# A mixture-of-experts kernel: three partial sums instead of four, base rows and fc2 fetched among the expert slots, each row turned ahead of the prior row's products

## The chip, the core and the metric

The kernel runs on one core of one Trainium2 chip. A core has five engines that run side by side, each with its own instruction queue: TensorE (PE, matrix products; its weight loads appear as PEld), VectorE (DVE), ScalarE (ACT), GpSimd (POOL) and SyncE (SP), which here only issues transfers. Sixteen DMA engines move data between the DRAM and the on-chip memory (128 partitions). The metric is the device time of one execution in microseconds (us); the median of three runs is given.

## What is computed

A sequence model layer on x of 4 rows of 512 tokens with 512 channels: a bidirectional decay scan (WKV), an attention-like time mix and channel mix, a second scan, and then a feed-forward part with 32 experts, of which each token uses 8. The change touches only how the experts' results are summed and added in. In the reference:

```python
# x: tokens x 512; topi, wsel: the 8 experts of each token and their weights
cw = zeros((T, E)).at[arange(T)[:, None], topi].add(wsel)
x_lat = x @ fc1_w.T                                  # 256 wide
h = relu2(einsum('tl,eil->eti', x_lat, w1))
h = h * cw.T[:, :, None]
y_lat = einsum('eti,eli->tl', h, w2)
routed = y_lat @ fc2_w.T                             # 512 wide
shared = relu2(x @ shared_up_w.T) @ shared_down_w.T
return shared + routed
```

The layer's output is x plus this. The kernel holds everything that is added to `routed` (x, the mixes and `shared`) in DRAM as `base_dram`, four rows of 512 tokens, transposed: channels on the partitions.

## The kernel before

**Order of the work.** From 0 to about 757 us the scans, the mixes, the routing and the shared expert run; their instruction orders are written out by hand. The routing scatters each token's latent row once per chosen expert into `x_dram`, grouped by expert (line 672), with the token's number in the last column. Then come the expert slots, then the end. Within the slots only VectorE's order is written by hand; in the end no engine's is. Elsewhere a scheduler places instructions by priority (program order) and readiness, and it may move a transfer far ahead of its place in the program where SP has nothing more urgent.

**The slots** (`pairs`, line 1148). A pair is two tiles of 128 rows. `fetch` (line 1058) loads the rows as `xg` on SP, into a ring of six buffers: the first 16 pairs (`MIXED`) by two loads, later ones by one. `slots` (line 1105) runs a pair through four steps, and three pairs are in work at a time: turn `xg` on TensorE and copy it to `xt`; first product (`h_ps`) and relu; square; second product (`y_ps`), scaled by the routing weight into `yo` (line 1138). GpSimd then adds each of the two tiles of 128 rows of 256 values to a sum in DRAM by an indirect DMA that accumulates (line 1140). There are four sums (`SUMS`), and pair i, tile j goes to sum (2i + j) mod 4. A scatter waits until the one before it on the same sum has landed. Padding rows carry token numbers from `ROWS` on, so they land behind the 2048 real rows. 74 pairs always run (`SURE`); six more lie in a conditional block (line 1166), which these inputs skip. The branch not taken makes up the semaphores that the block would have counted, on GpSimd after all scatters have landed (an instruction that ends at 1065.14 us).

**The end** (line 1171). `fc2` and three base rows are loaded (lines 1172 to 1177; the fourth's buffer holds expert weights until the slots are over). For each of four rows b: four loads of the sums (line 1186, tokens spread so that partition p gets tokens p, 128 + p, 256 + p, 384 + p, hence 1 KB pieces), three additions (line 1192), eight turnings on TensorE (`lt`, line 1196), a copy to `yl` by ScalarE (line 1200), sixteen products with `fc2` (line 99, called from 1205), two additions of the base (line 1207), two stores (line 1208).

**Where the buffers lie.** The pool `ep` of the slots begins where the pools `cpool` and `bp` of the earlier stages lay, and a buffer of it may be written once what was there is no longer used. The offsets in bytes within a partition, as the program of before has them:

| earlier stage | slots and end |
|---|---|
| `z` 153568 to 161760 | `xg`, six buffers, 153568 to 167560 (pair 0: 153568) |
| `lat`, two, 161760 to 171024 | |
| `side` 171040 to 191520 | `xt`, two: 167584 and 169632 to 171680 |
| | `ht` 171680, `hr` 175776 (two each), `yo` 179872 (six) to 192160 |
| `rstd` 191520 to 193568 | `index`, nine, 192160 to 192448 |
| `sh` 193568 to 201760 | `w1`, two: 192448 and 194496; `fc2` 196544 |
| `fg`, small ones, `sw`, `zeros`, tables: 201760 to 228384 | `base0` 200640, `base1` 208832, `base2` 217024 to 225216 |

A tag's buffers stand together, and `w1` is first asked for at pair 16. `side` holds intermediate results of the shared expert for the last rows and is stored by ScalarE's queue at 751.3 and 758.2 us (line 721). The profile leaves out digits at the end of names: `w1` is `w`, `fc2` is `fc`, and `base0` is `base`.

Of the kernel before, what the change touches and what calls it, by code (L numbers as in the profile page):

```python
# [29 lines left out]
F32 = mybir.dt.float32  # L30
AF = mybir.ActivationFunctionType
ALU = mybir.AluOpType
# [3 lines left out]
B = 4  # L36
# [13 lines left out]
SURE = 74  # L50
MIXED = 16
WIDTH = 256 + E + 1
SUMS = 4
EXP30 = math.exp(30.0)
UNIT = NC * T

# [9 lines left out]
def model_kernel(ctx: ExitStack, tc: tile.TileContext, a: dict, out: bass.AP):  # L66
# [200 lines left out]

    x_dram = dram.tile([E * REGION + 3 * P, WIDTH], F32, tag="x_dram", name="x_dram")

    sum_dram = [dram.tile([ROWS + P, 256], F32, tag=f"sum{i}", name=f"sum{i}") for i in range(SUMS)]  # L270


    z_dram = [dram.tile([NC, P, T], F32, tag=f"z{b}", name=f"z{b}") for b in range(B)]
# [482 lines left out]
    def clear_tails():  # L756


        zeros = bp.tile([P, WIDTH], F32, tag="zeros", name="zeros")
        nc.vector.memset(zeros, 0.0)  # L760
        nc.gpsimd.iota(
            zeros[:, 256 + E : 257 + E], [[0, 1]], base=ROWS, channel_multiplier=1,
            allow_small_or_imprecise_dtypes=True,
        )
        for i in range(3):

            if i < 2:
                spare = x_dram[E * REGION : E * REGION + 2 * P, :].rearrange("(p j) n -> j p n", j=2)[i]
            else:
                spare = x_dram[E * REGION + 2 * P :, :]  # L770
            s = nc.gpsimd.dma_start(spare, zeros)
            tc.declare_no_dep(s.ins, group="scatter", reason="no two write one row")
            tc.add_to_no_dep_group("scatter", s.ins)
        yield
        ps = acc_tile()
        nc.tensor.matmul(ps[:1, 0, :E], lhsT=ones[:, 0:1], rhs=seen, start=True, stop=True)
        tail = bp.tile([1, E], F32, tag="tail", name="tail")
        nc.vector.tensor_tensor(tail, ps[:1, 0, :E], region[:1, :], ALU.add)
        ends = bp.tile([1, E], mybir.dt.int32, tag="ends", name="ends")
        nc.vector.tensor_scalar(ends, tail, -1.0, None, ALU.add)  # L780
        yield
        for e in range(E):
            _, (row,) = nc.values_load_multi_w_load_instructions(
                ends[0:1, e : e + 1], engines=[mybir.EngineType.SP], min_val=0, max_val=E * REGION,
                skip_runtime_bounds_check_because="a region has room for every row and a slot's tail",
            )
            s = nc.sync.dma_start(x_dram[bass.ds(row, P), :], zeros)
            tc.declare_no_dep(s.ins, group="scatter", reason="no two write one row but with zeros")
            tc.add_to_no_dep_group("scatter", s.ins)
            if e % 4 == 3:  # L790
                yield
# [112 lines left out]
    def clear_sum(i, j):  # L904

        s = sum_dram[i]
        if j < 2:
            nc.sync.dma_start(s[j * ROWS // 2 : (j + 1) * ROWS // 2, :].rearrange("(p r) n -> p (r n)", p=P), zero)
        else:
            nc.sync.dma_start(s[ROWS:, :], zero[:, :256])  # L910

    sums = iter([(i, j) for j in range(3) for i in range(SUMS)])

# [124 lines left out]
    with (  # L1038
# [19 lines left out]
        def fetch(i):  # L1058
            xg = ep.tile([P, 2, WIDTH], F32, tag="xg", name="xg", bufs=6)
            rows = of_pair(2, i, ET.SP, E * REGION)  # L1060
            if i < MIXED:
                for j, row in enumerate(rows):
                    nc.sync.dma_start(xg[:, j, :], x_dram[bass.ds(row, P), :])
            else:

                nc.sync.dma_start(xg, x_dram[bass.ds(rows[0], 2 * P), :].rearrange("(p j) n -> p j n", j=2))
            return xg
# [37 lines left out]
        def slots(i, xg):  # L1105
            ps = turn(xg, "xt_ps")
            xt = tile4("xt", [2, 2, P])
            if i < MIXED:
                nc.vector.tensor_copy(xt, ps)  # L1109
            else:  # L1110
                nc.scalar.copy(xt, ps)

                w1 = tile4("w1", [2, 256])
                o = of_pair(0, i, ET.Activation, (E - 1) * (UNIT // 2))[0]
                nc.scalar.copy(w1.rearrange("p k n -> p (k n)"), big[:, bass.ds(o, 512)])  # L1115
            yield
            at = of_pair(0, i, ET.PE, (E - 1) * (UNIT // 2))
            h = tile4("ht", [2, 2, P])
            if i < MIXED:
                ps = rows_times(xt, at, 0, "h_ps")  # L1120
                r = tile4("hr", [2, 256])
                nc.scalar.activation(r, ps, AF.Relu)
                yield
                ps = turn(r, "ht_ps")
                nc.scalar.activation(h, ps, AF.Square)
            else:
                ps = inner(xt, w1)
                r = tile4("hr", [2, 256])
                nc.scalar.activation(r, ps.rearrange("p m j r -> p m (j r)"), AF.Relu)  # L1129
                yield  # L1130
                nc.vector.tensor_tensor(h.rearrange("p m j r -> p m (j r)"), r, r, ALU.mult)  # L1131
            yield
            ps = rows_times(h, at, 1, "y_ps")
            y = tile4("yo", [2, 256], bufs=6)
            index = ep.tile([P, 2], mybir.dt.uint32, tag="index", name="index", bufs=9)
            nc.vector.tensor_copy(index, xg[:, :, 256 + E])
            for j, column in enumerate(of_pair(1, i, ET.DVE, 256 + E - 1)):
                nc.vector.tensor_scalar(y[:, j, :], ps[:, j, :], xg[:, j, bass.ds(column, 1)], None, ALU.mult)  # L1138

                nc.gpsimd.indirect_dma_start(  # L1140
                    out=sum_dram[(2 * i + j) % SUMS][:, :],
                    out_offset=bass.IndirectOffsetOnAxis(ap=index[:, j : j + 1], axis=0),
                    in_=y[:, j, :], in_offset=None,
                    bounds_check=ROWS + P - 1, compute_op=ALU.add,
                )
            yield

        def pairs(first, end):

            live = []  # L1150
            with tc.manual_schedule(engines={ET.DVE}):
                for i in range(first, end + 3):
                    if i < end:
                        live.append(slots(i, fetch(i)))
                    for s in live:
                        next(s, None)
                    if len(live) > 3:
                        live.pop(0)
# [9 lines left out]
        slot_psum.close()  # L1168


        fc2 = tile4("fc2", [2, C], bufs=1)
        nc.sync.dma_start(fc2, a["fc2"])
        base = []
        for b in range(B):
            base.append(tile4(f"base{b}", [NC, T], bufs=1) if b + 1 < B else chunked(views(13, UNIT, 1)[0]))
            if b + 1 < B:
                nc.sync.dma_start(base[b], base_dram[b][:, :, :].rearrange("c p t -> p c t"))
        got = Ring([v.rearrange("p (t n) -> p t n", t=NT) for v in views(1, NT * 256, 4 * SUMS)])
        lat_t = Ring([chunked(v, 2) for v in views(10, 2 * T, 2)])
        res_ring = Ring([chunked(v, 2) for v in views(11, 2 * T, 4)])  # L1180
        with tc.tile_pool(name="fpsum", bufs=2, space=bass.MemoryType.PSUM, reuse_waits="tile") as fps:
            for b in range(B):
                parts = []
                for s in sum_dram:
                    g = got()
                    nc.sync.dma_start(g, s[b * T : (b + 1) * T, :].rearrange("(t p) n -> p t n", p=P))
                    parts.append(g)
                if b + 1 == B:
                    nc.sync.dma_start(base[b], base_dram[b][:, :, :].rearrange("c p t -> p c t"))
                while len(parts) > 1:  # L1190
                    for i in range(len(parts) // 2):
                        nc.vector.tensor_tensor(parts[i], parts[i], parts.pop(), ALU.add)
                ps = fps.tile([P, 2, T], F32, tag="lt", name="lt")
                for t in range(NT):
                    for k in range(2):
                        nc.tensor.transpose(
                            ps[:, k, t * P : (t + 1) * P], parts[0][:, t, k * P : (k + 1) * P], ident
                        )
                yl = lat_t()
                nc.scalar.copy(yl, ps)  # L1200
                for j in range(2):
                    ps = fps.tile([P, 2, T], F32, tag="ps", name="ps")
                    for i in range(2):
                        o = (2 * j + i) * P
                        product(ps[:, i, :], lambda k: fc2[:, k, o : o + P], lambda k: yl[:, k, :], 2)
                    res = res_ring()
                    nc.vector.tensor_tensor(res, base[b][:, 2 * j : 2 * j + 2, :], ps, ALU.add)
                    nc.sync.dma_start(out[b, 2 * j : 2 * j + 2].rearrange("c p t -> p c t"), res)


# [40 lines left out]
```

## Time and profile before

| | us |
|---|---|
| median of three runs | 1117.57 (1117.12 to 1117.61) |
| profiled execution, whole run | 1123.07 |
| its span (first to last instruction) | 1121.3 |
| TensorE busy | 1021.8 (91%) |
| VectorE busy | 678.9 (61%) |
| ScalarE busy | 469.7 (42%) |
| GpSimd busy | 406.2 (36%) |

The profile is of one execution, and its times are those of that execution, counted from the start of its span. A row gives an instruction group with what it writes and reads, how often, and its time; "idle before" is what its engine waited for just ahead of it. The granted clock is the share of TensorE's full speed that it was given. Some stretches, with busy time of TensorE and GpSimd:

| stretch, us | TensorE | GpSimd | granted clock | DMA share |
|---|---|---|---|---|
| 0 to 740 | 673.6 | 167.9 | 0.99 | 0.62 |
| 780 to 820 | 40.0 | 28.6 | 1.00 | 0.94 |
| 940 to 980 | 40.0 | 33.9 | 1.00 | 0.84 |
| 1042 to 1065 | 13.1 | 16.8 | 0.89 | 0.60 |
| 1065 to 1080 | 2.5 | 0 | 0.50 | 0.97 |
| 1080 to 1122 | 32.8 | 0 | 0.95 | 0.64 |

### The profile page before, as it was taken

The numbers are of one execution on the slowest core, as the hardware profiler recorded it, in microseconds if no ns is written. First come the engines' busy times: TensorE is split into PE (matmuls) and PEld (weight loads), VectorE is DVE, ScalarE is ACT, GpSimd is POOL, SyncE is SP. The second block draws the span as 40 slices with busy tenths as digits, with TensorE's granted clock in tenths as the row PEclk, the third lists the DMA queues.
The fourth block names the chain that finished last, engine by engine and source line by source line (L and its number), as shares of the span: only waits on it lengthen the run. The fifth ranks groups of instructions, "written<-read, shape, count | busy, mean of one in ns | idle before, by whom it ended". The sixth has DMA issues, their size and how long they took to land.

```text
span 1121.3 us, 11548 instructions
## 1 busy us (share of the span) xinstructions
PE 1021.8 (91%) x3284; PEld 587.8 (52%) x3284; DVE 678.9 (61%) x1194; ACT 469.7 (42%) x671; POOL 406.2 (36%) x350
## 2 busy tenths in 40 slices
PE   2569899999999989999997999999999999999657
PEld 0124344444444434544453544447888888888523
DVE  7899799999897798439429632114444434433343
ACT  4464764864764655345225220202234444344100
POOL 3000000000000000335466635504778888888700
PEclk9989999999999999999999999999999999999969
DMA  3614374967347426754897669976978888888695
GB/s 129 252 47 177 122 210 175 342 173 207 126 107 234 164 103 178 255 140 139 245 325 268 214 207 289 295 219 164 225 132 143 146 146 144 141 145 150 70 283 204
DMA packets 105912, 208.41 MB, mean 186 GB/s; under 512 B 10836, under 2 KB 55384, under 8 KB 101176
## 3 DMA queue, kind: packets, MB, share of 16 engines
q1 hardware_dynamic: 71576, 152.07, 40.7%
q0 software_dynamic: 33728, 54.53, 26.6%
q10 hardware_dynamic: 544, 1.05, 0.2%
q8 instruction: 29, 0.48, 0.2%
q14 instruction: 35, 0.29, 0.1%
HBM read 126.87 MB, written 84.94 MB: 189 GB/s over the span
## 4 chain that ended last, share of the span: by engine, by line
PE 59%; DVE 27%; ACT 6%; DMA 5%; issue 3%; POOL 0%; SPq 0%; DVEq 0%; ACTq 0%; POOLq 0%
PE ps L99 21%; PE ps L489 12%; PE y_ps L1088 11%; PE h_ps L1099 8%; PE xt_ps L1077 3%; PE h_ps L1088 2%; DVE side L358 2%; DVE big L358 2%; DVE side L344 2%; DVE big L344 2%; DVE big L454 2%; DMA sum<-yo,index 2%; DMA big<-base 2%; ACT big L450 1%; DVE big L427 1%
## 5 line engine op out<-in xcount | busy, mean ns | idle before, releaser
L489 PE MATMUL ps<-big 128*128 128x512 f32 x896 | 393.1, 598 | 17.2 <-DVE big L454 6.7
L489 PEld LDWEIGHTS ps<-big 128*128 128x128 f32 x896 | 170.9, 192 | 235.7 <-issue 212.1
L1140 POOL DMA_INDIRECT sum<-yo,index x148 | 238.3, 1610 | 96.9 <-DVE yo L1138 73.6
L1138 DVE TENSOR_SCALAR yo<-y_ps,xg 128x256 f32<-128x256 f32 x148 | 64.8, 480 | 149.0 <-PE y_ps L1088 149.0
L672 POOL DMA_INDIRECT x_dram<-lat,index x128 | 139.2, 1087 | 42.9 <-issue 33.5
L1088 PE MATMUL y_ps<-big,ht 128*128 x592 | 140.2, 380 | 1.6 <-DVE ht L1131 1.6
L525 POOL DMA_DIRECT2D base<-big x8 | 10.6, 1324 | 319.9 <-DVE big L519 200.6
L1088 PEld LDWEIGHTS y_ps<-big,ht 128*128 128x128 f32 x592 | 106.7, 190 | 13.7 <-DVE ht L1131 2.2
L99 PE MATMUL ps<-big,sw 128*128 128x512 f32 x256 | 112.2, 593 | 1.5 <-ACT side L309 1.5
L1099 PE MATMUL h_ps<-xt,w 128*128 128x256 f32 x464 | 109.6, 379 | 0.0
L1099 PEld LDWEIGHTS h_ps<-xt,w 128*128 128x128 f32 x464 | 88.1, 190 | 11.9
L1129 ACT ACTIVATE hr<-h_ps 128x512 f32<-128x512 f32 x58 | 34.6, 597 | 132.0 <-PE h_ps L1099 129.7
L99 PEld LDWEIGHTS ps<-big,sw 128*128 128x128 f32 x256 | 48.3, 190 | 60.6 <-issue 57.6
L450 ACT ACTIVATE big<-big,vec,prior_g 128x511 f32<-128x511 f32 x80 | 58.4, 802 | 27.8 <-DVE big L443 27.8
L363 ACT ACTIVATE side<-side,tiny 128x512 f32<-128x512 f32 x32 | 23.1, 721 | 102.5 <-DVE side L360 102.4
L99 PE MATMUL ps<-sh,sw 128*128 128x512 f32 x128 | 56.7, 595 | 3.7 <-ACT sh L732 3.7
L454 DVE SCALAR_TENSOR_TENSOR big<-big,own_g 128x512 f32<-128x512 f32 x80 | 55.7, 748 | 0.3
L743 DVE TENSOR_TENSOR big<-big,ps 128x1024 f32<-128x1024 f32 x10 | 12.2, 1220 | 63.5 <-PE ps L99 33.8
L1115 ACT COPY w<-big 128x512 f32 x58 | 36.1, 622 | 28.3 <-DVE xt L1109 27.8
L358 DVE TENSOR_TENSOR_SCAN side<-decay,side 128x512 f32<-128x512 f32 x32 | 39.0, 1218 | 13.8 <-ACT side L345 13.8
L1077 PE MATMUL xt_ps<-ident,xg 128*128 128x128 f32 x296 | 44.2, 273 | 0.0
L345 ACT ACTIVATE side<-side,rest 128x511 f32<-128x511 f32 x32 | 23.0, 718 | 48.9 <-DVE side L344 48.8
(235 smaller groups left out, 1281.3 us busy)
## 6 DMA issues: line engine op xcount, KB each, us to landing
xg<-x_dram SPq DMA_DIRECT2D x58, 289.0 KB
big<-in_w SPq DMA_DIRECT2D x32, 512.0 KB
ekx<-side SPq DMA_DIRECT2D x16, 512.0 KB
base<-big POOLq DMA_DIRECT2D x8, 1024.0 KB
sum<-big SPq DMA_DIRECT2D x8, 1024.0 KB
side<-ekx SPq DMA_DIRECT2D x16, 512.0 KB
big<-sum SPq DMA_DIRECT2D x16, 512.0 KB
side<-in_side SPq DMA_DIRECT2D x22, 256.0 KB
```

The costliest lines, as they stand in the source:

```text
L99: done[0] = nc.tensor.matmul(dst, lhsT=lhs(k), rhs=rhs(k), start=(k == 0), stop=(k == n - 1))
L344: nc.vector.tensor_tensor_scan(f, decb, data, 0.0, ALU.mult, ALU.add)
L358: nc.vector.tensor_tensor_scan(f[:, ::-1], decb, f[:, ::-1], 0.0, ALU.mult, ALU.add)
L450: nc.scalar.activation(m[:, c, 1:], xc[:, c, : T - 1], AF.Identity, bias=col(f"L0_attn_{which}_b", c), scale=prior_g[mu][:, c : c + 1],)
L454: nc.vector.scalar_tensor_tensor(m[:, c, :], xc[:, c, :], own_g[mu][:, c : c + 1], m[:, c, :], ALU.mult, ALU.add)
L489: done[0] = nc.tensor.matmul(ps[:, i, :], lhsT=w[:, k, f * P : (f + 1) * P], rhs=m[:, k, :], start=(k == 0), stop=(k == NC - 1),)
L672: s = nc.gpsimd.indirect_dma_start(out=x_dram[:, :], out_offset=bass.IndirectOffsetOnAxis(ap=index[:, i : i + 1], axis=0), in_=lats[:, t, ...
L1077: nc.tensor.transpose(ps[:, k, j, :], src[:, j, k * P : (k + 1) * P], ident)
L1088: nc.tensor.matmul(ps[:, j, :], lhsT=src[:, k, j, :], rhs=weights(at[j], of, k), start=(k == 0), stop=(k == 1),)
L1099: nc.tensor.matmul(ps[:, m, :, :], lhsT=w[:, k, m * P : (m + 1) * P], rhs=src[:, k, :, :], start=(k == 0), stop=(k == 1),)
L1138: nc.vector.tensor_scalar(y[:, j, :], ps[:, j, :], xg[:, j, bass.ds(column, 1)], None, ALU.mult)
L1140: nc.gpsimd.indirect_dma_start(out=sum_dram[(2 * i + j) % SUMS][:, :], out_offset=bass.IndirectOffsetOnAxis(ap=index[:, j : j + 1], axis=0 ...
```

## The change

- `SUMS` is 3. Each sum gets 256 rows for padding instead of 128. Mixed pairs use sum (2i + j) mod 3. From pair 16 on both tiles of a pair go to sum i mod 3, and the two scatters need not wait for each other; for that the second of the two tiles of padding gets token numbers of its own (`other`).
- The sums are loaded so that a partition gets four tokens in a row (4 KB in one piece). The turned row then has its tokens in another order, and the copy to `yl` puts them back with a stride of four.
- `fc2` and the base rows are asked for ahead of the slots. The base is held as eight halves: seven of their own, the eighth in the old place. Their loads stand in the program among the pairs, one at each fourth pair from 20 on; the eighth half is still loaded in the end.
- In the end the order of TensorE is written by hand: row b + 1 is turned ahead of row b's products.
- The very last addition and store are cut in two.

```diff
-SUMS = 4
+SUMS = 3
...
-    sum_dram = [dram.tile([ROWS + P, 256], F32, tag=f"sum{i}", name=f"sum{i}") for i in range(SUMS)]
+    sum_dram = [dram.tile([ROWS + 2 * P, 256], F32, tag=f"sum{i}", name=f"sum{i}") for i in range(SUMS)]
...
+        other = bp.tile([P, 1], F32, tag="other", name="other")
+        nc.gpsimd.iota(
+            other, [[0, 1]], base=ROWS + P, channel_multiplier=1, allow_small_or_imprecise_dtypes=True,
+        )
...
+            parts = [(spare, zeros)]
+            if i == 1:
+                parts = [(spare[:, : 256 + E], zeros[:, : 256 + E]), (spare[:, 256 + E :], other)]
+            for dst, src in parts:
+                s = nc.gpsimd.dma_start(dst, src)
...
-                nc.gpsimd.indirect_dma_start(
-                    out=sum_dram[(2 * i + j) % SUMS][:, :],
+                s = nc.gpsimd.indirect_dma_start(
+                    out=sum_dram[(2 * i + j if i < MIXED else i) % SUMS][:, :],
...
+                if i >= MIXED:
+                    tc.declare_no_dep(s.ins, group=f"pair{i}", reason="rows of one expert")
+                    tc.add_to_no_dep_group(f"pair{i}", s.ins)
             yield
+        fc2 = tile4("fc2", [2, C], bufs=1)
+        base = [
+            [
+                tile4(f"base{b}{j}", [2, T], bufs=1) if (b, j) < (B - 1, 1) else chunked(views(13, 2 * T, 1)[0], 2)
+                for j in range(2)
+            ]
+            for b in range(B)
+        ]
+        early = [(base[b][j], base_dram[b][s].rearrange("c p t -> p c t")) for b in range(B) for j, s in enumerate(halves)]
+        early = early[:-1] + [(fc2, a["fc2"])]
...
                     if i < end:
                         live.append(slots(i, fetch(i)))
+                    if i > MIXED and i % 4 == 0 and early:
+                        nc.sync.dma_start(*early.pop(0))
...
-                    nc.sync.dma_start(g, s[b * T : (b + 1) * T, :].rearrange("(t p) n -> p t n", p=P))
+                    nc.sync.dma_start(g, s[b * T : (b + 1) * T, :].rearrange("(p t) n -> p t n", t=NT))
...
-                nc.scalar.copy(yl, ps)
...
+                nc.scalar.copy(
+                    yl.rearrange("q k (p t) -> q k t p", t=NT), ps.rearrange("q k (t p) -> q k t p", t=NT)
+                )
+                return yl
+            with tc.manual_schedule(engines={ET.PE}):
+                coming = turned(0)
+                for b in range(B):
+                    yl = coming
+                    coming = turned(b + 1) if b + 1 < B else None
+                    for j in range(2):
...
+                        for s in ((0, 1), (1, 2)) if (b, j) == (B - 1, 1) else ((0, 2),):
+                            s = slice(*s)
+                            nc.vector.tensor_tensor(res[:, s, :], base[b][j][:, s, :], ps[:, s, :], ALU.add)
+                            o = slice(2 * j + s.start, 2 * j + s.stop)
+                            nc.sync.dma_start(out[b, o].rearrange("c p t -> p c t"), res[:, s, :])
```

## The prediction

> **What bounds the kernel now.** I read the page's chain of waits first. Its shares say that TensorE sets most of the time:
>
> ```profile
> PE 59%; DVE 27%; ACT 6%; DMA 5%; issue 3%; POOL 0%; SPq 0%; DVEq 0%; ACTq 0%; POOLq 0%
> ```
>
> The change touches the expert slots (from 757 us) and what follows them, so I then read the chain in order of time at three places (columns: start, length in us, what). Here the shared part ends and the slots begin:
>
> ```profile
> 739.73 17.18 PE ps L99 x40
> 756.93 1.23 DVE side L743
> 758.19 2.78 DMA base<-side
> ...
> 761.26 0.70 DVE xt L1109
> ...
> 762.01 1.13 PE h_ps L1088 x4
> ```
>
> The last addition into `side` and its store delay pair 1: its copy into `xt` starts 0.3 us after the store has landed, although the second `xt` buffer only borders on `side` (table of offsets). So a new tile waits until the whole old tile under it is free. From 762.01 the chain is unbroken TensorE to 1040: 4.33 us per mixed pair, 3.89 per later one. Then the end:
>
> ```profile
> 1046.89 18.25 DMA sum<-yo,index
> ...
> 1066.87 6.77 DMA big<-sum
> ...
> 1076.30 1.95 PE lt L1196 x8
> ...
> 1078.34 1.02 ACT big L1200
> ...
> 1079.40 6.00 PE ps L99 x8
> ...
> 1097.92 0.89 PE lt L1196 x8
> ...
> 1098.89 1.02 ACT big L1200
> ...
> 1099.95 7.13 PE ps L99 x16
> ```
>
> TensorE stands from 1056.7 to 1076.3, waiting for the scatters, the loads of the sums and their additions. Then each row of tokens costs 7.13 (products) + 0.89 (turning) + about 1.1 (the copy by ScalarE, in which TensorE idles). Last I read the queues' timelines, and stretches with the granted clock as last but two number:
>
> ```profile
> 747.48 29.70 SPq L1063 DMA_DIRECT2D xg<-x_dram  x18
> 777.31 0.33 SPq L1172 DMA_DIRECT2D fc<-in_fc  x1
> 777.70 0.43 SPq L1177 DMA_DIRECT2D base<-base  x1
> ```
>
> ```profile
> 70.00:71.00 1.00, 0.00 (x0) 0.00 (x0) 1.00 (x2) 0.40 (x1) 0.00 (x0) 0.64 0.00 0
> 71.00:77.00 6.00, 4.64 (x6) 2.04 (x7) 5.95 (x9) 6.00 (x11) 0.00 (x0) 0.50 0.00 1
> 77.00:78.00 1.00, 1.00 (x3) 0.51 (x3) 0.95 (x3) 1.00 (x3) 0.00 (x0) 0.95 0.00 0
> ```
>
> The first fence: `fc2` and three of four base rows are already loaded during the slots, and pair 0's `xg` is fetched at 747.5, nine microseconds ahead of use. The second: after TensorE had stopped at 65.6, the clock was halved at 70.3; work resumed at 72.4 and had the full clock at 77.05.
>
> **Loads in the slots: nothing gained, but the buffers move.** `fc2` and `base` are now asked for before the first `xg`. The table shows that the pool lays its tags out in the order of first request (`w1`, first asked for at pair 16, lies behind `index`). So `fc2` takes 153568 to 157664, seven halves of 4096 bytes reach to 186336, and the six `xg` buffers follow, 2336 apart. Before, pair 0 got the first `xg` buffer; that is now 186336 to 188648, inside `side` (171040 to 191520). Its load must wait for the last store of `side`, which lands at 760.97, and on SP every other fetch is queued behind it.
>
> - Fetch: two loads at 761.0 and 761.55 (before: 747.48 and 748.04). A load issued at 760.99 moved its data from 761.85 to 762.95, so I put landing at 2.1 us after issue: 763.1 and 763.65. Pair 1 follows at SP's spacing of 1.9 us, landing near 765.5.
> - Turning to 764.2, copy 0.7 to 764.9, `h_ps` of pair 0 (1.73) to 766.6; with pair 1's turning and its late data between, `h_ps` of pair 1 starts near 767.7. Before, it started at 762.01 and ran on unbroken: **+5.7**, bounds +4.7 (pair 1 fetched first) and +6.3.
> - Clock: TensorE now idles from 756.9 to 763.1, 6.2 us. The rows: after a gap of 6.7 us half clock for 4.7 us of work; after one of 4.7 us (55.8 to 60.5) for 2.9 us. Half of each is lost: 2.35 or 1.45; I take **+1.9**, bounds 0 and 2.4. The Trainium skill (TensorE: Matmul & The Clock Gate, Part 1) speaks against such a gap: one idle window of about 3.4 us halves the clock, and 3.4 us of sustained work restore it. By the rule the loss is 1.7, by the rows 1.9; the sum moves by 0.2.
>
> Start of the slots: +7.6. Nothing later absorbs it, since TensorE is then the bound. The base loads themselves stay on SP in gaps behind the first fetches: before, 3.5 MB went there with TensorE 40.0 of 40 us busy (780 to 820), now 4 MB; I take nothing, bound +1 if a fetch queues behind several of them.
>
> **Three sums, GpSimd.** A scatter is an indirect DMA of 1.56 us plus at least 0.30 between two, so a pair costs 3.73 against TensorE's 3.89:
>
> ```profile
> 857.60 1.56 POOL L1140 DMA_INDIRECT sum<-yo,index  x1 [0.30 <-issue]
> 859.63 1.56 POOL L1140 DMA_INDIRECT sum<-yo,index  x1 [0.47 <-DVE yo L1138]
> ```
>
> The slack is 0.17 per pair. The last scatter started at 1060.26 and GpSimd's waits for all scatters were over by 1064.3, so a scatter lands at most 4.0 after its start. In the mixed pairs a scatter now waits for the third before it, started 6.2 earlier: no wait. From pair 16 on both scatters of a pair go to one sum, last used three pairs (11.7 us) earlier: no wait, except once at pair 16, whose sum was used by the scatter just before: 4.0 - 1.86 = 2.1 us, made up in some 13 pairs behind six `yo` buffers. Cost 0; bound +3 if waits pile up. Nine clearings instead of twelve (TensorE waits for none between 154 and 234 us), one more index column and one small DMA by GpSimd near 11 us (the three there take 0.54 to 0.81, and GpSimd is then idle until 145): 0.
>
> **The end.** The loads still start only after the last scatter has landed and the branch not taken has been made up on GpSimd (until 1065.14): unchanged. I work in before's times.
>
> - Four loads of 0.524 MB ran at 348 GB/s from about 1066.9; the last addition was released at 1073.64. Three loads with 4 KB per partition: 1.573 MB. No 4 KB row exists; the near row is a store of 2 KB rows, 389 GB/s at 759.2 to 760.2. The Trainium skill (DMA: Bandwidth & Descriptors, Specifications) puts line rate at 512 B and above, so 1 KB rows would lose nothing. By the row a set takes 4.04, by the rule 4.52; I take the row, since 348 and 389 are both measured here. Set 0 is in at 1071.65, set 1 at 1075.7 (rule: 1076.65).
> - Two additions after the last landing, 1.24 each. The turning of row 1 now stands ahead of row 0's products: 1075.7 + 2.48 + 0.14 + 1.95 (half clock) = 1080.3, where before products began at 1079.40: **+0.9** (rule +1.8). The strided copy of row 0 (contiguous: 1.02; bound 2.0) is done by 1078.5: hidden.
> - Row 0's products again 9.41 with the cold start, bound 1 less because the turning comes just ahead: to 1089.7. Then 0.89 + 7.13 + 0.89 + 7.13 + 7.13 = 23.2, to 1112.9, against 1116.25: the three copies (1.10, 1.16, 1.16) are gone, and one turning (0.89) already lies ahead of row 0's products. TensorE ends **-3.35**. Sets 2 and 3 are in by 1084: no wait. Without that cover a late set is paid in full.
> - The last half in two: addition 0.6 instead of 1.22; the last store 0.26 MB at 385 GB/s, 0.68 instead of 1.36: **-1.3**.
>
> End: -4.6, bounds -3.4 and -5.8.
>
> **Sum.** +7.6 - 4.6 = +3.0. The profiled execution (span 1121.3, run 1123.07, so 1.8 outside) stands 5.5 above the median of 1117.57; I carry the difference over: 1117.57 + 3.0 = **1120.6**, own range 1116.5 to 1122.9.
>
> **Rivals.**
> 1. *No delay at the start* (not slower): pair 0's load goes to a buffer outside `side`, or its wait is placed behind other fetches. For it: buffers 4 to 6 lie in `rstd` and `sh`, `sh` free at 750. Against it: pair 0 took the first buffer before, and `xt` shows whole-tile waits. Then only the end counts: 1117.57 - 4.6 = 1113.0. It decides as soon as the delay is under 4.6 us.
> 2. *The clock stays full* over the 6.2 us: +5.7 - 4.6, 1118.7, within 0.2%. Against it: both gaps above.
> 3. *GpSimd becomes the bound* in pairs 16 to 73: beyond 0.17 us more per pair, every further 0.1 costs 58 x 0.1 = 5.8 us; at 0.27 it is 1120.6 + 5.8 = 1126.4. Against it: the second scatter of a pair should need no new wait.
> The change doing less than it says is no rival but part of the sum: the early loads were already there.
>
> **Chances.** A measurement of this kernel can tell 0.2% (2.2 us) from no change. Forecast 0.70, of which 0.50 lies above +2.2 and 0.20 within; rival 1: 0.15; rival 2: 0.09; rival 3: 0.06. So faster 0.15, same 0.29, slower 0.56. The range goes from rival 1's value, with the better end bound of the tail, to just above the forecast's own range.
>
> **What would show it.** Right: the first `xg` fetch near 761 instead of 747.5, with SP waiting for the store of `side`; TensorE idle about 6 us at 757, half clock after it, the first `y_ps` some 7 us later; turning of row 1 directly behind that of row 0, and no ScalarE gap between later rows; about 51 us from the first sum load to the end of the span instead of 56. Wrong: a first fetch before 755, GpSimd behind the pairs with waits on scatters, or row 1's sums landing later than 1076 + 7.6.

## The result and the profile after

The kernel after takes 1122.19 us (median of 7 runs, 1119.96 to 1123.14), the kernel before, run beside it, 1118.5 (7 runs, 1117.12 to 1119.97). The ratio is 1.0032, 95% interval 1.0021 to 1.0044: slower by 3.6 us (2.3 to 4.9). The profiled execution of after took 1122.19 as a whole, its span 1120.4.

The two profiled spans differ by -0.9, the medians by +3.7. Up to the end of the shared expert's products (call it S) the change touches only the clearing of the sums and one index column, and that end lies anywhere from 750.7 to 756.9 us in the profiles of this study (before 756.90, after 752.36). So all that follows is counted from S, over four marks that every profile has:

| stretch | before | after | difference | predicted |
|---|---|---|---|---|
| S to the first `y_ps` product | 7.82 | 16.28 | +8.46 | +7.6 |
| first to end of the last `y_ps` | 291.96 | 291.96 | 0 | 0 |
| end of the last `y_ps` to the first load of a sum | 8.61 | 10.34 | +1.73 | 0 |
| first load of a sum to the end of the span | 56.01 | 49.46 | -6.55 | -4.6 |
| sum | | | +3.64 | +3.0 |

**The start.** Timeline of after (columns: start, length, engine, line, what, count, idle time of the engine just before and what ended it):

```profile
756.61 9.05 SPq L1072 DMA_DIRECT2D xg<-x_dram  x12
758.96 1.09 PE L1086 MATMUL xt_ps<-ident,xg 128*128 128x128 f32 x4 [6.60 <-DMA xg<-x_dram]
760.15 0.69 DVE L1118 COPY xt<-xt_ps 128x512 f32<-128x512 f32 x1 [6.53 <-PE xt_ps L1086]
760.50 1.22 PE L1086 MATMUL xt_ps<-ident,xg 128*128 128x128 f32 x4 [0.46 <-DMA xg<-x_dram]
762.18 4.88 PE L1097 MATMUL h_ps<-big,xt 128*128 x12 [0.46 <-DMA xg<-x_dram]
```

The first rows are asked for at 756.61, 4.25 after S (before: 9.4 ahead of S), and TensorE stands 6.60 for them. The second turning is pair 1's: its rows are asked for 1.63 after pair 0's, and pair 0's first product (762.18) stands behind it in TensorE's queue, though pair 0's copy into `xt` is done at 760.84. Before has the same order, the turnings of both pairs (eight instructions) and then the product (758.81):

```profile
756.74 1.04 PE L1077 MATMUL xt_ps<-ident,xg 128*128 128x128 f32 x8
```

Who held the fetch is in SP's waits (columns: for what, us in total, times, longest):

```profile
SPq L1072 <- DMA base<-side: 13.6, 2, 6.8
```

It is the store of `side`. The pool is made with `reuse_waits="tile"` in both kernels; whether a finer wait would have let the load go ahead was not tried. In stretches of 2 us, with the granted clock as the last figure but two:

```profile
754.00:756.00 2.00, 0.00 (x0) 0.00 (x0) 0.00 (x0) 0.80 (x2) 0.00 (x0) 1.00 0.67 262
756.00:758.00 2.00, 0.00 (x0) 0.00 (x0) 0.00 (x0) 0.44 (x1) 0.00 (x0) 0.53 0.13 21
...
764.00:766.00 2.00, 2.00 (x6) 1.62 (x5) 0.00 (x0) 0.03 (x1) 0.00 (x0) 0.50 0.62 154
766.00:768.00 2.00, 2.00 (x12) 1.71 (x12) 0.00 (x0) 1.03 (x2) 0.00 (x0) 0.91 0.90 227
```

The clock falls to one half at 756.1 and comes back at 766.3, so nearly all of the twelve products that make up pair 0's first product and half of pair 1's run at half speed (4.88 in all).

**GpSimd at pair 16.** Its timeline:

```profile
838.16 1.56 POOL L1150 DMA_INDIRECT sum<-yo,index  x1 [0.30 <-issue]
843.96 1.56 POOL L1150 DMA_INDIRECT sum<-yo,index  x1 [4.24 <-DVE yo L1147]
```

The row at 843.96 is pair 16's first scatter. It starts 5.80 after the one ahead of it, which adds into the same sum; in before the two stood 2.03 apart. The view names `yo`, but `yo` was there at 839.92: it waits for the scatter ahead to land. The same line of the program from 838.1 to 843.9, with the instructions of GpSimd's queue (columns: how often, shortest, median and longest in ns, first and last start in us):

```profile
L1150 POOL DMA_INDIRECT sum<-yo,index x1: 1557/1557/1557, 838.2 to 838.2; - x1
L1150 POOLq EVENT_SEMAPHORE  x1: 17/17/17, 842.0 to 842.0; - x1
L1150 POOLq MOVE  x1: 29/29/29, 843.7 to 843.7; - x1
...
DMA to landing us min/median/max: 3.8/3.8/3.8
```

The scatter ahead landed 3.8 after its start, and the wait for it (`EVENT_SEMAPHORE`) ended at 842.0. The next scatter started 2.0 later still; for 1.8 of that the trace shows nothing. In `e5_both`, an experiment below in which this scatter waits for no such landing, the same two instructions stand as far apart, mostly beside the scatter ahead:

```profile
L1150 POOLq EVENT_SEMAPHORE  x1: 17/17/17, 829.3 to 829.3; - x1
L1150 POOLq MOVE  x1: 29/29/29, 831.1 to 831.1; - x1
```

So the stall is a landing and then 2.0 of the queue's own time, which the wait brings into the open. What GpSimd does in that time stays open; at three such waits in the first pairs a scatter started 0.7 to 0.8 behind the landing. GpSimd is now 3.8 behind, two scatters. The same view 28 us later:

```profile
871.90 1.58 POOL L1150 DMA_INDIRECT sum<-yo,index  x1 [0.30 <-DMA sum<-yo,index]
...
875.65 1.72 POOL L1150 DMA_INDIRECT sum<-yo,index  x1 [0.30 <-DMA sum<-yo,index]
```

Up to here a pair took 3.72, and GpSimd made up 0.17 in each. From 875.65 on one scatter of each pair takes 1.72 or 1.73, a pair takes 3.89, and GpSimd is in step with TensorE, still one scatter behind. All 47 long scatters of after start about 0.4 behind the start of VectorE's squaring, and from pair 16 on none of the others starts so near behind it (a later pair):

```profile
929.76 0.68 DVE L1140 TENSOR_TENSOR ht<-hr 128x512 f32<-128x512 f32 x1
930.14 1.73 POOL L1150 DMA_INDIRECT sum<-yo,index  x1 [0.31 <-DVE yo L1147]
```

Before has the same step and the same 1.73, but there it is the first scatter of a pair, and in after the second. The last scatter starts 5.44 after the last `y_ps` (before: 3.58), 1.86 later: one scatter.

**The end.**

```profile
1077.60 2.49 DVE L1215 TENSOR_TENSOR big<-big 128x1024 f32<-128x1024 f32 x2 [16.08 <-DMA big<-sum]
1080.23 1.94 PE L1219 MATMUL lt<-ident,big 128*128 128x128 f32 x8 [19.62 <-DVE big L1215]
1081.40 2.48 DVE L1215 TENSOR_TENSOR big<-big 128x1024 f32<-128x1024 f32 x2 [1.31 <-DMA big<-sum]
1082.27 2.01 ACT L1223 COPY big<-lt 128x1024 f32<-128x1024 f32 x1 [26.42 <-PE lt L1219]
1084.03 1.94 PE L1219 MATMUL lt<-ident,big 128*128 128x128 f32 x8 [1.86 <-DVE big L1215]
1085.17 2.49 DVE L1215 TENSOR_TENSOR big<-big 128x1024 f32<-128x1024 f32 x2 [1.29 <-DMA big<-sum]
1085.76 7.75 PE L99 MATMUL ps<-big,fc 128*128 128x512 f32 x16
...
1093.35 1.04 PE L1219 MATMUL lt<-ident,big 128*128 128x128 f32 x8
1094.22 7.03 PE L99 MATMUL ps<-big,fc 128*128 128x512 f32 x16
...
1101.96 13.90 PE L99 MATMUL ps<-big,fc 128*128 128x512 f32 x32
...
1115.90 1.29 DVE L1243 TENSOR_TENSOR big<-big,ps 128x512 f32<-128x512 f32 x2 [2.21 <-PE ps L99]
```

A set of three loads comes every 3.8 us (additions at 1077.60, 1081.40, 1085.17). Row 1 is turned ahead of row 0's products, and from 1084.03 TensorE runs without a gap to 1115.86; no ScalarE copy stands between rows any more, though a copy now takes 2.01. The last row shows the halved addition: neither half starts before the last product has ended.

### The profile page after: what moved, and what is told of

It is laid out like the page before. It is cut to its first block, busy times and chain, and to the rows that moved or that the text cites. A ratio compares the mean times of both kernels' runs of the same rounds, so it can differ in the third digit from the quotient of the medians.

```text
span 1120.4 us, 11489 instructions
## 1 busy us (share of the span) xinstructions
PE 1023.2 (91%) x3284; PEld 589.9 (53%) x3284; DVE 670.3 (60%) x1191; ACT 474.2 (42%) x671; POOL 407.5 (36%) x352
## 5 line engine op out<-in xcount | busy, mean ns | idle before, releaser
L525 POOL DMA_DIRECT2D base<-big x8 | 10.6, 1324 | 319.9 <-DVE big L519 200.9
L1086 PEld LDWEIGHTS xt_ps<-ident,xg 128*128 128x128 f32 x296 | 37.2, 142 | 15.9 <-issue 7.4
```

Source lines behind the costliest of these rows:

```text
L1086: nc.tensor.transpose(ps[:, k, j, :], src[:, j, k * P : (k + 1) * P], ident)
```

## The experiments

All times of a run are set against before, run beside it on the same chip. The table has them all; the stretches are those of the first table, from each kernel's profile.

| kernel | median, us | ratio to before (95%) | S to first y | y to first load | first load to end |
|---|---|---|---|---|---|
| after | 1122.19 | 1.0032 (1.0021 to 1.0044) | 16.28 | 10.34 | 49.46 |
| e1_old_layout | 1112.27 | 0.9958 (0.9947 to 0.9970) | 7.62 | 10.22 | 49.69 |
| e2_before_layout | 1124.88 | 1.0064 (1.0038 to 1.0090) | 16.40 | 8.52 | 55.73 |
| e3_next_sum | 1119.33 | 1.0021 (1.0010 to 1.0032) | 15.80 | 8.45 | 49.99 |
| e4_warm | 1123.22 | 1.0051 (1.0033 to 1.0070) | 17.20 | 10.23 | 50.62 |
| e5_both | 1112.85 | 0.9951 (0.9933 to 0.9969) | 7.62 | 8.48 | 50.72 |
| e6_not_ahead | 1132.36 | 1.0122 (1.0097 to 1.0148) | 16.24 | 12.20 | 57.32 |
| e7_one_kb | 1124.34 | 1.0059 (1.0037 to 1.0080) | 15.95 | 10.25 | 51.58 |
| e8_warm26 | 1123.38 | 1.0047 (1.0029 to 1.0065) | 14.65 | 10.31 | 50.24 |
| e9_four_sums | 1122.50 | 1.0027 (1.0016 to 1.0038) | 16.98 | 8.40 | 51.89 |
| e10_warm_end | 1111.94 | 0.9937 (0.9923 to 0.9951) | 7.63 | 9.04 | 49.18 |

From the first to the end of the last `y_ps` each of them took 291.96 to 291.98.

### The place of the rows, taken out of after and put into before

`e1_old_layout` is the kernel after, with the tiles asked for late:

```diff
+        def ask():
             fc2 = tile4("fc2", [2, C], bufs=1)
...
             early.extend(...)
...
+                    if i == MIXED + 3:
+                        ask()
```

> The kernel after, with one thing put back: the tiles of fc2 and of the base rows are asked for only once pair 18 is done, so that the slot's rows come to lie where they lay before, and pair 0's fetch is no longer laid over the shared expert's up products. Theory (the delay at the start is the place of pair 0's rows, and nothing else): the first fc2 products of pair 0 end about 8 us behind the shared expert's products instead of 16.28, TensorE's granted clock doesn't fall to 0.5, and the time falls by 8.5 to about 1113.7. Rival (the base loads in the pairs, the three sums or the scatters make the loss, and the start is only where it shows): the time stays within 1.5 of 1122. Between them (a part of the start made up later, because the scatters set the end): 1116 to 1119.

`e2_before_layout` is the kernel before, with the requests moved ahead of the pairs and nothing else:

```diff
+        fc2 = tile4("fc2", [2, C], bufs=1)
+        base = [tile4(f"base{b}", [NC, T], bufs=1) for b in range(B - 1)] + [chunked(views(13, UNIT, 1)[0])]
...
         def pairs(first, end):
```

> The kernel before, with one thing of the change alone: the tiles of fc2 and of the base rows are asked for ahead of the pairs; their loads stay where they were. Theory: pair 0's rows then lie over the shared expert's up products, their fetch starts only when the side's products are done, the first fc2 products of pair 0 end about 16 us behind the shared expert's products instead of 7.82, and the time rises by about 8.5 to about 1127. Rival (the place of the rows costs nothing; the delay comes from the loads that were moved into the pairs): no change, 1117 to 1120.

Measured: 7.62 instead of 16.28 in the one, 16.40 instead of 7.82 in the other. The ratio goes from 1.0032 to 0.9958, 8.3 us down, and from 1 to 1.0064, 7.2 us up. The start of `e2_before_layout`, whose loads stand where before had them:

```profile
759.51 15.34 SPq L1063 DMA_DIRECT2D xg<-x_dram  x13
761.87 1.17 PE L1077 MATMUL xt_ps<-ident,xg 128*128 128x128 f32 x4 [6.69 <-DMA xg<-x_dram]
```

and of `e1_old_layout`, whose base loads stand in the pairs as in after:

```profile
743.78 11.90 SPq L1072 DMA_DIRECT2D xg<-x_dram  x6
...
751.13 1.04 PE L1086 MATMUL xt_ps<-ident,xg 128*128 128x128 f32 x8
```

In the second TensorE turns pair 0's rows with no idle time ahead of it, right behind the shared expert. Requests for memory, which are no instructions on any engine, make the whole loss at the start. The loads in the pairs cost nothing, and none of the 8.3 is made up later.

### The stall at pair 16

`e3_next_sum` changes one index:

```diff
-                    out=sum_dram[(2 * i + j if i < MIXED else i) % SUMS][:, :],
+                    out=sum_dram[(2 * i + j if i < MIXED else i + 1) % SUMS][:, :],
```

> The kernel after, with the pairs from 16 on taking the sums in an order moved on by one, so that pair 16 no longer adds into the sum that the scatter just ahead of it is adding into. Theory (one stall of about 3.8 us at pair 16's scatter puts GpSimd one scatter behind, and it never makes that up): the stall at pair 16 is gone, the last scatter starts about 2 us behind the last y instead of 4.5, the way from the last fc2 products to the first load of a sum falls from 10.34 to about 8.6, and the time falls by 1.7 to about 1120.5. Rival (the lag is from the mixed pairs' own waits on their sums, or from scatters that are longer by themselves): no change, within 0.6 of 1122.

The same spot on GpSimd, pair 16's first scatter at 838.29:

```profile
838.29 2.01 POOL L1150 DMA_INDIRECT sum<-yo,index  x1 [0.60 <-DVE yo L1147]
```

The wait ahead of it is 0.60 instead of 4.24, and the stretch behind the last `y_ps` is 8.45 instead of 10.34, so -1.9 where -1.7 was expected. The waits in the mixed pairs are still there and cost nothing; the rival falls. The ratio's gain, 0.0011, is 1.2 us, but the two intervals overlap: the mechanism is shown by the profile, its size in the whole time only roughly.

### Both repairs

> The kernel after with both repairs: fc2's and the base rows' tiles asked for behind pair 18, and the pairs from 16 on taking the sums moved on by one. Theory (the two losses are independent: 8.3 from the place of pair 0's rows, 1.7 from GpSimd's lag): products' end to the first fc2 products 7.7, last fc2 products to the first load of a sum 8.5, and the time is some 10 below after, about 1111, 6 to 6.5 below before. Rival (with an earlier start the scatters are the bound again, so the two repairs overlap): no faster than with the late tiles alone, 1112.5 or more.

Both stretches are repaired (7.62 and 8.48), as the theory says, and `e5_both` beats before by 5.5 us (3.5 to 7.5). Its median, 1112.85, misses the theory's 1111 and meets the rival's mark (1112.5 or more). Against `e1_old_layout`, 0.9951 to 0.9958, the second repair can't be told from nothing. In the profile of `e5_both` the last stretch was 1.0 longer, as the first set landed 7.4 after its first load instead of 6.2. So the sum of the two gains shows in the stretches and is open in the medians.

### The clock at the start

`e4_warm` adds products that nobody reads behind the shared expert:

```diff
+    with tc.manual_schedule(engines={ET.PE}):
+        warm = acc_tile()
+        for _ in range(50):
+            nc.tensor.matmul(warm[:, 0, :P], lhsT=ones, rhs=ident, start=True, stop=True)
```

> The kernel after, with 50 products of 128x128 added on TensorE between the shared expert and pair 0's first turning, whose result nobody reads. Theory (about 2 us of the loss at the start is the clock: TensorE stands idle for 6.6 us, is granted half its clock, and works pair 0's first products at it): the idle time before the first turning falls to under 3 us, the granted clock stays at 1.0 from 758 to 766, the first 12 products take about 2.5 us instead of 4.88, and the time falls by 2 to about 1120. Rival (the chain at the start is set by the fetch of the rows and the slower products lie beside it): no change, within 0.6 of 1122; or the added products push the first turning back, and it rises.

A miss: I had guessed the length of the added products. They took 11.33 and ended 11.2 after S, some 4.5 behind the landing of the rows. The clock did stay at 1.00, and the first twelve products took 2.86 instead of 4.88, so most of the delay was won back (17.20 instead of 16.28), but nothing was gained:

```profile
763.40 2.86 PE L1101 MATMUL h_ps<-big,xt 128*128 x12 [0.41 <-DVE xt L1122]
...
767.87 1.89 PE L1101 MATMUL y_ps<-big,ht 128*128 x8
```

`e8_warm26` has 26 of them.

> The kernel after with 26 added products in the place of the 50 of the earlier run, whose 11.3 us reached past the coming in of pair 0's rows by some 4.7. At 0.227 for each they take 5.9 and end just ahead of the rows, which came 6.6 after the shared expert's end. Theory (the half clock costs about 2 on the chain of the start): TensorE's granted clock stays at 1.0, the first 12 products take about 2.9 instead of 4.9, from the shared expert's end to the first fc2 products are 14 to 14.5 instead of 16.3, and the time falls by 2 to about 1119 to 1119.5. Rival (the fetch sets the start and the slower products lie beside it): 16 to 16.5 at the start, and no change.

```profile
754.38 5.97 PE L1047 MATMUL ps<-ident,ones 128*128 128x128 f32 x52
761.25 0.85 PE L1090 MATMUL xt_ps<-ident,xg 128*128 128x128 f32 x4 [0.91 <-DMA xg<-x_dram]
762.70 0.44 PE L1090 MATMUL xt_ps<-ident,xg 128*128 128x128 f32 x2 [0.60 <-DMA xg<-x_dram]
763.96 1.97 PE L1101 MATMUL h_ps<-big,xt 128*128 x8 [0.81 <-DMA xg<-x_dram]
```

At the full clock the first `y_ps` comes 14.65 after S, 1.63 sooner than in after. That is not the clock's alone, since here half of pair 1's turning stands behind pair 0's first product. `e4_warm` has after's order: from pair 0's first product to the first `y_ps` it took 4.47 at the full clock, in after 6.46, so 2.0. The half clock was thus worth 1.6 to 2.0, and the remaining 6.5 to 6.8 over before are the late fetch and what follows from it. These are single profiles: the other kernels with after's start show 15.80 to 16.98 to the first `y_ps`. The whole time doesn't show the 1.63 (the intervals of 1.0047 and 1.0032 overlap; from S to the end of the span it is 367.2 against 368.0).

### The parts of the gain at the end

`e6_not_ahead` turns each row only in its turn:

```diff
-                coming = turned(0)
...
-                    yl = coming
-                    coming = turned(b + 1) if b + 1 < B else None
+                    yl = turned(b)
```

> The kernel after, with each row turned only when its turn comes and not beside the prior row's products; the loads by four tokens per partition and everything else as in after. Theory (the turning ahead takes the turning and the ScalarE copy of 2.0 out of the chain three times): products of row 0 may start some 1.4 sooner, as they no longer wait for row 1's turning, but behind each of the three other rows TensorE then waits some 2.1 for a copy, and the end is about 5 longer: first load to end 54 to 55, time about 1126. Rival (the sets' arrival sets the end, and the turning ahead adds nothing): within 1 of after, first load to end 49 to 50.

```profile
1088.29 9.52 PE L99 MATMUL ps<-big,fc 128*128 128x512 f32 x16 [2.13 <-ACT big L1223]
...
1100.74 7.13 PE L99 MATMUL ps<-big,fc 128*128 128x512 f32 x16 [2.05 <-ACT big L1223]
```

The direction is right, the size too small: from the end of row 0's products to the end of row 3's it took 30.28 (1097.81 to 1128.09), in after 22.35, in before 27.44. So turning ahead gives 2.64 per row with the strided copy, and against before's shorter copy 1.70. The stretch before it, 12.20, shows how the lag at pair 16 is kept. The stall is the same (4.18), but here GpSimd is in step at once, with nothing made up, and stays two scatters behind:

```profile
846.64 2.07 POOL L1150 DMA_INDIRECT sum<-yo,index  x1 [4.18 <-DVE yo L1147]
849.02 1.56 POOL L1150 DMA_INDIRECT sum<-yo,index  x1 [0.30 <-issue]
850.88 1.73 POOL L1150 DMA_INDIRECT sum<-yo,index  x1 [0.30 <-DVE yo L1147]
```

Nothing of this part of the program differs from after. The stretches 8.61, 10.34 and 12.20 stand 1.7 to 1.9 apart, none, one and two scatters. I take the number to depend on how GpSimd and VectorE stand to each other behind the stall; that was not tried.

`e7_one_kb` loads the sums in 1 KB rows again:

```diff
-                    ... .rearrange("(p t) n -> p t n", t=NT))
+                    ... .rearrange("(t p) n -> p t n", p=P))
...
-                nc.scalar.copy(
-                    yl.rearrange("q k (p t) -> q k t p", t=NT), ps.rearrange("q k (t p) -> q k t p", t=NT)
-                )
+                nc.scalar.copy(yl, ps)
```

> The kernel after, with the sums loaded as before, in rows of 1 KB, and the contiguous ScalarE copy; the turning ahead stays. Theory (the wide rows bring a set every 3.8 where the 1 KB rows bring one every 4.5, and row 1's turning waits for the second set): the products of row 0 start some 1.5 later, the copy of 1.0 in the place of 2.0 gives nothing, as it lies beside products, and the time rises by 1.5 to about 1122.5 to 1123. Rival (the size of the row is of no account, since the rate was held down in before by something else beside it): within 0.6 of after.

```profile
1078.07 2.48 DVE L1215 TENSOR_TENSOR big<-big 128x1024 f32<-128x1024 f32 x2 [16.38 <-DMA big<-sum]
1082.56 2.48 DVE L1215 TENSOR_TENSOR big<-big 128x1024 f32<-128x1024 f32 x2 [2.01 <-DMA big<-sum]
...
1086.92 8.73 PE L99 MATMUL ps<-big,fc 128*128 128x512 f32 x16
1087.00 2.48 DVE L1215 TENSOR_TENSOR big<-big 128x1024 f32<-128x1024 f32 x2 [1.96 <-DMA big<-sum]
```

A set now takes 4.49 and 4.44 instead of 3.80 and 3.77, and row 0's products start 15.90 after the first load instead of 14.82: the wide rows are worth 1.1 there, and the stretch is 2.1 longer in all, of which 1.0 is in row 0's products (8.73). The rival, that something beside the loads held the rate down in before, falls by these stretches; the medians alone would not settle it (the intervals of 1.0059 and 1.0032 overlap).

`e9_four_sums` is after with `SUMS = 4`.

> The kernel after with four sums in the place of three; all else as in after. With four, pair 16's first sum is not the one that pair 15's last scatter adds into. Theory (three sums save a load and an addition in each row's set, and cost the stall at pair 16): the stall of 4.2 ahead of pair 16's scatter is gone and the way from the last fc2 products to the first load of a sum is 8.5 in the place of 10.34; from there a set takes 5.05 in the place of 3.8 and an addition of 1.24 more, so row 1's turning, behind two sets, is 2.5 to 3.7 later, first load to end is 52 to 53.2 in the place of 49.5, and the time about 1 to 2 above after. Rival (three sums bring nothing, since sets and additions lie beside products): first load to end 49.5 to 50, and the time 1.8 below after. A second rival (with a sum more, no scatter of a mixed pair waits either): the same at the end, and no wait of a scatter on another at all.

The stall at pair 16 is gone (0.60), no scatter waits for another, the stretch behind the last `y_ps` is 8.40, and the last stretch 51.89. So three sums give 2.4 at the end and take 1.9 on GpSimd, and the time is after's (1.0027 against 1.0032, the intervals overlap). Both the theory and the second rival hold in part: the end pays for four, and the waits go.

### Keeping the clock up ahead of the end

`e10_warm_end` is `e5_both` with

```diff
+                warm = fps.tile([P, 2, T], F32, tag="ps", name="ps")
+                for _ in range(76):
+                    nc.tensor.matmul(warm[:, 0, :P], lhsT=ones, rhs=ident, start=True, stop=True)
                 coming = turned(0)
```

> The kernel with both repairs (late tiles, sums moved on by one), and 76 products of 128x128 more on TensorE between the last pair's fc2 products and the first turning of a row; nobody reads them. TensorE stands idle there for 18.5; at 0.227 for each they take 17.3. Theory (TensorE's clock falls in the idle time, and the turnings and the first row's products run at it): the turnings of rows 0 and 1 take 1.04 in the place of 1.94, of which the second lies on the chain, the first row's 16 products 7.0 in the place of 8.25; the end is about 2 shorter and the time about 1110.5 to 1111. Rival (the sets' arrival sets the end of the row's chain, or the time is made up elsewhere): within 0.6 of the kernel with both repairs. Or the added products push the first turning back: longer by what they reach past it.

The first turning took 1.09 instead of 1.94, the second 1.40, but row 0's products 8.46. In stretches:

```profile
1070.00:1074.00 4.00, 1.28 (x12) 1.04 (x11) 2.45 (x2) 2.00 (x1) 0.00 (x0) 1.00 1.03 411
1074.00:1075.00 1.00, 1.00 (x7) 1.00 (x6) 0.27 (x1) 0.05 (x1) 0.00 (x0) 0.58 1.04 414
1075.00:1076.00 1.00, 1.00 (x2) 0.38 (x2) 0.96 (x2) 1.00 (x1) 0.00 (x0) 0.50 1.00 397
...
1077.00:1078.00 1.00, 1.00 (x3) 0.48 (x2) 0.21 (x1) 0.00 (x0) 0.00 (x0) 0.72 0.98 387
```

Between the two turnings TensorE waits 2.72 for the second set, and the clock falls at 1074.2, when TensorE is already at work again, to come back 3.4 later (the last section says why). So the theory holds for the turnings and fails for the products. From the first load to the end it is 1.5 shorter than `e5_both`, from the last `y_ps` to the first load 0.6 longer. This is the lowest of all medians, 1111.94, 0.9937 of before (0.9923 to 0.9951), some 7 us below before and 10.6 below after; against `e5_both` alone the gain isn't certain.

## Why the prediction was right

The forecast was 1120.6, slower by 3.0; measured were 1122.19 and +3.6. The direction and its cause, pair 0's buffer over `side`, were right. The close sum is partly luck: three terms were mis-sized by 0.9, 1.7 and -1.95, and these cancel to 0.65.

- **Fetch, "+5.7": 6.5 to 6.8.** The first load came as predicted (4.25 after S, predicted 4.1), and it landed after 2.2 instead of 2.1. The size was off in TensorE's order: the prediction put pair 0's first product right behind pair 0's copy and pair 1's turning after it. In the queue pair 1's turning comes first and waits for pair 1's rows, so the product started at 762.18, 1.34 after the copy. That goes beyond the upper bound of 6.3. Before's trace already had this order.
- **Clock, "+1.9": 1.6 to 2.0** (`e8_warm26`, `e4_warm`). Both the rows' 1.9 and the rule's 1.7 (the Trainium skill, TensorE: Matmul & The Clock Gate, Part 1) lie within; the runs can't tell them apart. The rival in which the clock stays full is out, and so is the one without a delay.
- **Base loads in the slots, 0: right.** The stretch of the pairs is 291.96 with the loads in the pairs and with them where before has them.
- **GpSimd, "Cost 0": 1.73.** This step failed, and at two places. "A scatter lands at most 4.0 after its start" held at pair 16 (3.8), but the next scatter was taken to start at the landing, and it started 2.0 later. So the one wait was 3.9 (4.24 less the fixed gap of 0.3), not 2.1. And "made up in some 13 pairs" took the slack of 0.17 per pair as lasting. The slack was there for eight pairs; then GpSimd fell into step, 1.73 + 0.30 + 1.56 + 0.30 = 3.89, with one scatter still lost, and its last scatter sets when the sums may be read. The rival of a GpSimd that becomes the bound in the pairs did not come (the stretch of the pairs is 291.96); but its place, the thin slack, was the right one to suspect. In the first mixed pairs scatters do wait for the third before them, against "no wait": there a landing took 6.3 to 7.0, and three waits came to 1.3 to 1.5 each, without cost.
- **Sets of 4 KB, "4.04": 3.80.** The 4 KB rows ran at some 414 GB/s; 389 from the row was too low, and the rule's 4.52 (the Trainium skill, DMA: Bandwidth & Descriptors, Specifications) is what 1 KB rows take (4.47 in `e7_one_kb`). So the page's line rate from 512 B on did not hold here: 1 KB rows lose against 4 KB rows. Row 0's products came 14.82 after the first load, predicted 15.0.
- **Row 0's products, "9.41, bound 1 less": 7.75** in after, 7.97 to 9.09 in the other kernels that turn ahead and load 4 KB rows. In after the clock came back at 1087.2, within these products. The bound (8.4) was the better value.
- **The row series, "23.2": 22.35.** I added the turnings and products end to end; a turning begins 0.16 before the last product's modelled end, and the products without a gap take 6.87 a row.
- **The last half, "-1.3": -0.51.** From the last product to the end of the span it is 4.54 instead of 5.05. The two half additions stand from 1115.90 to 1117.19, behind the products of both halves, and take no less than the one of before (1.22). So only the store got shorter. The halves share one `ps` tile, and the addition waited for the whole of it, as `xt` did for `side` in the prediction's first view. That it is the tile was not tried.

## What to carry to other kernels

Asking for a buffer earlier moves every buffer behind it: before hoisting a request, lay the new offsets over what was there before, and look for the first load that now waits for the last store of an earlier stage. Reckon a wait for a transfer as the landing and what the waiting queue still has to do behind it (here 3.8 and 2.0), not as the landing alone, and count on a lag of an engine to be made up only if its slack per step is larger than the error of the rows that it is worked out from. Changes to one kernel can be a gain and a loss of the same size: this change holds a gain of 6.55 at the end, and a later request and another starting sum keep it.

## What the hardware did that was not expected

- The same ScalarE copy of 128x1024 values takes 2.01 with the outputs at a stride of four elements and 1.01 contiguous (`e7_one_kb`).
- Loads in 1 KB rows and in 4 KB rows differ by 18% in rate (4.47 against 3.78 for 1.573 MB) with nothing else moving.
- GpSimd's scatters fall into step with the pairs: one of each pair is stretched from 1.56 to 1.73, just so far that a pair takes TensorE's 3.89, and a lag of one or two whole scatters is then kept for 40 pairs and more. It starts 0.4 behind VectorE's squaring; whether that is what stretches it was not tried.
- TensorE's clock goes by stretches of fixed length. Within each of the twelve traces its changes lie whole multiples of 3.41 apart (after has half clock for 10.24 at the start of the slots and for 23.89 ahead of the end). Cut at these times, the traces show a fall behind each full-clock stretch of 3.41 in which TensorE was busy for 1.40 or less (over 70 of them), and behind none with 1.46 or more. The stretch ahead of the fall in `e10_warm_end`, and the one with the gaps of `e8_warm26` (columns: from and to, length, busy time of TensorE, weight loads, VectorE, ScalarE, GpSimd, then the granted clock):

```profile
1070.74:1074.15 3.41, 0.69 (x7) 0.64 (x7) 2.45 (x2) 2.00 (x1) 0.00 (x0) 1.00 1.03 411
```

```profile
761.88:765.29 3.41, 2.00 (x10) 1.44 (x9) 0.69 (x1) 0.00 (x0) 0.00 (x0) 1.00 0.75 209
```

So an idle time of 2.72 was enough in the first, while idle pieces of 0.60 and 0.81 in the second did not bring the clock down: by these traces it is the busy share of a stretch that counts, and not the length of one gap.
